# Half of a look-up's lowest-bit picks made by ScalarE in 16-bit halves, and second-level gate sums traced earlier

## The chip, the cores and the metric

The kernel runs on one core of one Trainium2 chip. The metric is the device time of one execution in microseconds (us). The engines are TensorE (PE in the profile, PEld for its weight loads), VectorE (DVE), ScalarE (ACT), GpSimd (POOL) and SyncE (SP). Each has its own list of instructions and works it off in order; "ACTq" and "SPq" in the profile are transfers issued from the lists of ScalarE and SyncE.

## The reference

The input x is 2 x 2048 x 512 in fp32. One block of a transformer is computed, attention first:

```
n = layernorm(x)
q, k, v = n Wq, n Wk, n Wv
s = softmax(q^T k / 4)          # per batch, 512 x 512: over features, not tokens
x = x + (s v^T)^T Wo
```

and then a feed-forward part whose weights are stored as indices into a table of 16 fp32 values:

```
n = layernorm(x)
g = n . lut[gate_idx]^T         # gate_idx and up_idx: 1376 x 512
u = n . lut[up_idx]^T
x = x + (silu(g) * u) . lut[down_idx]^T     # down_idx: 512 x 1376
```

So 3 x 1376 x 512 weights have to be looked up before they can be multiplied with. All products are in fp32.

## The kernel before

**Stages.** Attention over features needs only the 512 x 512 products n^T n of each batch, which the first stage (`gram`) accumulates from the 4096 tokens. Small products of 512 x 512 (`Square`, seven half-size products in place of eight, after Strassen and Winograd) turn them into one matrix m for each batch. Then come 32 blocks of 128 tokens in which y = n m is made: `y_product(k)` is four matmuls, the transposed normalised block nT(k) being their weights. After that `GateUp(f, p)` makes the gate and up products for 128 of the 1376 rows (f from 0 to 10) and 1024 tokens (p from 0 to 3), again in seven or so products a unit, and `Down` makes the last product.

**The order is written out by hand.** TensorE, VectorE, ScalarE and SyncE execute their instructions in the order in which the program's text calls them. What is called one after the other for one engine stays so on that engine, and an instruction that waits holds up all that is behind it on its engine.

**The y stage.** The loop over k calls, in this order: `n_turned(k + 1)` (VectorE transposes the next block, L738, so nT is made one block ahead), `y_product(k)`, `side(k)` and `pump`. `side(k)` calls `added(k - 1)`: VectorE adds y to x and sums the row (L761), ScalarE makes the mean (L164) and the sum of squares (L165, and a read of the accumulator) out of it; after each fourth block a root (L169). Then come, for an earlier block, the transposed copies of the second layernorm (L738 again, from k = 16 on), seven small VectorE operations that finish the layernorm of four blocks (once in four blocks), and `f_normed(k - 6)`: ScalarE normalises a block (L231), and after every second one issues the transfer that stores two of them (L220).

**The look-up.** A `Job` stands for 128 rows of one of the three index matrices, and there are 33 (g, u and wd, each 0 to 10), in a fixed order. ScalarE casts the indices to int16 (`cast`, L251), and VectorE does the rest: it masks out bits 1, 2 and 3 of the index (L263, L264, L269), spreads bit 0 over the word (L267), makes eight picks by bit 0 of the values of two neighbouring entries each, in one bitwise operation (L277), and joins them by seven predicated copies (L289), four of which go by bit 1, two by bit 2 and one by bit 3. `pump(us)` is called between TensorE's products and hands out as many of these operations as the given time allows, by written-down costs. So the pace of the look-up is set by where TensorE stands in the program's text.

**Gate and up units.** A unit calls a1, c1, extra1, the last unit's a4, a2, extra2, c2, b and a3 with `between()`, that is a pump, in between. a1 and c1 are copied out of PSUM by ScalarE (p1 at L932, p7 at L938), so is a2 (u2, L943); VectorE adds c2 to u2, makes the gate's sum h0, and c22 from the unit's accumulator and p7 (L135). ScalarE applies silu to h0 (L1002) and, after a4, to h1 (L1018). a4 of a unit is put between products of the next, and it overwrites the accumulator that c22 reads, so a4 waits for c22.

**Second level.** For f = 2 to 9 two neighbouring f share a second level of the same scheme. Its left sums, s1 to s4 of two gate blocks (`l2_left`, four VectorE operations on 128 x 128), are called ahead of unit (f, 1) for even f, and unit (f, 1)'s extra product into the PSUM tile x reads them.

```
if 1 < f < NFT - 1 and f % 2 == 0 and p == 1:
    for op in l2_left(f):
        op()
```

Of the kernel before, what the change touches and what calls it, by code (L numbers as in the profile page):

```python
# [48 lines left out]
F32 = mybir.dt.float32  # L49
BF16 = mybir.dt.bfloat16  # L50
I32 = mybir.dt.int32
I16 = mybir.dt.int16
# [14 lines left out]
def tile_attn_ffn(  # L67
# [43 lines left out]
    lut_sb = const.tile([P, NLUT], F32, tag="lut", name="lut_sb")  # L111
    lut_x = const.tile([P, NLUT // 2], I32, tag="lutx", name="lut_x")
    eps_sb = const.tile([P, 1], F32, tag="eps", name="eps_sb")
    lut_i = lut_sb.bitcast(I32)
    wd = wdp.tile([P, NFT, E], F32, tag="wd", name="wd")
    nd = dram.tile([NCH, P, KB, J, P], F32, tag="nd", name="nd")
# [21 lines left out]
    class Norm:  # L138
        def __init__(self, c, name, back=None):
            self.name, self.back = f"{name}{c}", back  # L140
            if back:
                self.std, self.mean = back.rstd, back.nmr
            self.rstd = const.tile([P, J], F32, tag=f"rstd_{self.name}", name=f"rstd_{self.name}")
            self.nmr = const.tile([P, J], F32, tag=f"nmr_{self.name}", name=f"nmr_{self.name}")
            self.minus, self.scale = -1.0, 1.0
# [90 lines left out]


    class Job:
        def __init__(self, name, rows, cols, load, dest, after, gate):
            self.name, self.rows, self.cols = name, rows, cols  # L240
            self.load, self.dest, self.after, self.gate = load, dest, after, gate
# [13 lines left out]
            return t[: self.rows, : self.cols]  # L255

        def ops(self):

            rows, f, idx, b3 = self.rows, self.cols / 1024, self.idx, self.b3
            vec = nc.vector  # L260
            w = self.dest()
            b1, b2 = self.bits("b1", 1), self.bits("b2", 1)
            vec.tensor_scalar(b1, b3, 2, None, ALU.bitwise_and)  # L263
            vec.tensor_scalar(b2, b3, 4, None, ALU.bitwise_and)  # L264
            yield 0.2 + 0.54 * f

            vec.tensor_scalar(idx, idx, 31, 31, ALU.logical_shift_left, ALU.arith_shift_right)  # L267
            yield 0.1 + 0.55 * f
            vec.tensor_scalar(b3, b3, 8, None, ALU.bitwise_and)  # L269
            yield 0.1 + 0.27 * f  # L270
            masks = [None, b1, b2, b3]

            def pick(level, at, dest):

                if level == 1:
                    k = at // 2
                    vec.tensor_scalar(  # L277
                        dest.bitcast(I32), idx, lut_x[:rows, k : k + 1],
                        lut_i[:rows, at : at + 1], ALU.bitwise_and, ALU.bitwise_xor,
                    )  # L280
                    yield 0.2 + 0.55 * f
                    return
                yield from pick(level - 1, at, dest)
                half = 1 << (level - 1)
                t = gub.tile(
                    [P, 512], F32, tag="pick", name=f"{self.name}_{level}_{at}", bufs=3
                )[:rows, : self.cols]
                yield from pick(level - 1, at + half, t)
                vec.copy_predicated(dest, masks[level - 1], t)  # L289
                yield 0.1 + 1.17 * f  # L290

            yield from pick(4, 0, w)
            yield from self.after()

# [62 lines left out]
        jobs += [gate_job(f), up_job(f), gate_job(f + 1), up_job(f + 1), down_job(5 + f // 2)]  # L357
    jobs += [gate_job(NFT - 1), up_job(NFT - 1), down_job(NFT - 1)]
    assert len(jobs) == 3 * NFT

    def looked_up():

# [11 lines left out]

    lookup = looked_up()
    owed = [0.0]

    def pump(us):

        owed[0] = min(owed[0] + us, 2 * us + 1.0)  # L380
        while owed[0] > 0:
            cost = next(lookup, None)
            if cost is None:
                return
            owed[0] -= cost
# [153 lines left out]
    for c in range(1, NCH):  # L539
        for j in range(J):  # L540
            gram(c, j)
            if c in (CPB - 1, CPB + 1, CPB + 2):
                n_stored()
            if c == 1 and j == 0:
                second(2)
            if c + 1 < NCH and j < 2:
                for i in (2 * j, 2 * j + 1):
                    ln1[c + 1].stats(i, xc[c + 1][:, i, :])
            elif c + 1 < NCH and j == 2:
                ln1[c + 1].sqrt(0, J)  # L550
                pump(0.6)
                ln1[c + 1].rest(0, J)
                pump(0.6)
            elif ahead and c > STORED + 2:
                for op in ahead[:4]:
                    op()
                del ahead[:4]
            else:
                pump(1.9)
            if c == 1 and j == 1:  # L560
                nc.vector.tensor_tensor(
                    lut_x, lut_pairs[:, :, 0], lut_pairs[:, :, 1], ALU.bitwise_xor
                )
            if c == CPB and j == 1:
                gram_out(0)
            if c == CPB + 1 and j == 3:
                wk_sb = load_weight(wk, "a0", "wk_sb")
                wq_sb = load_weight(wq, "a1", "wq_sb")
                wk_ops = right(wk_sb, "wk")
                ahead += wk_ops.todo  # L570
            if c == CPB and j == 3:
                copies = gram_mirror(0)
            if c == CPB + 1 and j == 1:
                for copy in copies:
                    copy()
                g_ops = [left(gs[0], "g_0")]
                ahead += g_ops[0].todo
# [262 lines left out]
    for k in range(NBLK):  # L840
        if k:
            n_turned(k + 1)
        y_product(k)
        if k == 0:
            before[0].a4()
            n_turned(1)
            n_load(1)
        else:
            if k % J == 3 and k // J + 2 < NCH:
                n_load(k // J + 2)  # L850
            side(k)
        pump(1.6 if k < LAG else 1.0)
    pps.release()
    sums.release()
    ffn = tc.alloc_tile_pool(name="ffn", bufs=1, reuse_waits="tile")
# [19 lines left out]
    def l2_left(f):  # L875


        t = wgu.tile([P, 4, P], F32, tag="l", name=f"l_{f}", bufs=1)
        if f == NFT - 1:
            a12 = gu[f]["12"]  # L880
            both, minus = (t[:, q, : FT[f][1]] for q in range(2))
            gu[f]["both"], gu[f]["minus"] = both, minus
            return [
                lambda: add(both, a12[:, 0, :], a12[:, 1, :]),
                lambda: nc.vector.tensor_scalar_mul(minus, a12[:, 0, :], -1.0),
            ]
        a11, a12 = gw[f][:, 2, :], gw[f][:, 3, :]
        a21, a22 = gw[f + 1][:, 2, :], gw[f + 1][:, 3, :]
        s1, s2, s3, s4 = (t[:, q, :] for q in range(4))
        l2a[f // 2] = {"22": a22, "S1": s1, "S2": s2, "S3": s3, "S4": s4}  # L890
        return [
            lambda: add(s1, a21, a22), lambda: sub(s2, s1, a11),
            lambda: sub(s3, a11, a21), lambda: sub(s4, a12, s2),
        ]
# [11 lines left out]
    class GateUp:  # L906
# [14 lines left out]
        def temp(self, tag, bufs=1):  # L921
            t = ffn.tile([P, CH], F32, tag=tag, name=f"{tag}_{self.name}", bufs=bufs)
            return t[: self.rows, :]
# [100 lines left out]
    class Line:  # L1024
# [29 lines left out]
        def flush(self):  # L1054
            self.last.a4()
            self.last.end()
            self.last = None

    todo = []

    def between():
        if todo:
            todo.pop(0)()
            pump(0.3)
        else:
            pump(1.0)

# [192 lines left out]
    for f, p in units:  # L1260
        while f not in gu or 1 < f < NFT - 1 and p and (f | 1) not in whole:
            next(lookup)
        assert p in xs
        if 1 < f < NFT - 1 and f % 2 == 0 and p == 1:
            for op in l2_left(f):
                op()
        if f == NFT - 1 and p == 0:
            assert not todo and next(lookup, None) is None
            x2p.release()
            gub.release()  # L1270
            for name in ("hp0", "dT"):
                hps[name] = tc.alloc_tile_pool(
                    name=name, bufs=1, side="right", reuse_waits="tile"
                )
            hps[0] = hps["hp0"]
            h = Hidden(0)
            todo += by_two(l2_left(f) + down_sums(hps["dT"]))
        if f == NFT - 1 and p == 1:
            h.rest_of()
            todo += by_two(h.sums())  # L1280
        if f == NFT - 1 and p == 3:
            units = [Down(h, 0)]
        line.run(GateUp(f, p), final=(f, p) == (NFT - 1, NPR - 1))
        if p == NPR - 1:
            passed[0] = f + 1
        if (f, p) == (1, 1):
            xnp.release()
            x2p = tc.alloc_tile_pool(name="x2p", bufs=1, side="right", reuse_waits="tile")
        if f == 1 and p % 2:
            todo += l2_sums(p // 2)  # L1290
# [84 lines left out]
```

## Time and profile before

| | us |
|---|---|
| median of 3 runs (lowest, highest) | 1086.42 (1086.38, 1086.46) |
| the profiled execution | 1086.16 |
| its span, first to last instruction | 1084.2 |
| TensorE busy in it | 1076.2 |
| VectorE busy | 769.2 |
| ScalarE busy | 331.2 |
| GpSimd busy | 35.6 |

The granted TensorE clock is 1.000 over the span. By stage, from the trace: up to 178 us (gram and squares) VectorE is busy for 140.5 us and ScalarE for 75.8; from 178 to 292 us (the y stage) for 100.6 and 60.0 of 114; from 292 to 790 us (gate and up) for 418.6 and 148.4 of 498; after that (down) for 109.5 and 47.0 of 294. TensorE's idle time over the whole span is 8.0 us.

A line of the groups names a line of the program, the engine and operation, output and inputs, shape and count; then the busy time in all and the mean of one in ns; then the engine's idle time just before these instructions and what ended it. A line of the timeline has the start, the duration, the engine and the operation, and in brackets the idle time before it. Durations overlap: an instruction's successor on VectorE or ScalarE often starts before the reported end.

### The profile page before, as it was taken

What the parts mean: (1) busy time and instruction counts of PE and PEld (TensorE: products, weight loads), DVE (VectorE), ACT (ScalarE), POOL (GpSimd) and SP (SyncE); (2) the same over time, 40 slices, a digit from 0 to 9 for tenths busy, and PEclk for the clock granted to TensorE, in tenths of its full rate; (3) what the DMA queues carried; (4) which work ended last, traced back from release to release, by engine and by line L of the source; (5) the groups of instructions that cost most, each with busy time, mean ns of one, the idle gap of its engine ahead of it and who ended that gap; (6) DMA issues with size and microseconds to landing.
All of it is one profiled execution on the core that took longest, in us unless ns stands there. A gap on an engine that the chain in (4) does not pass through costs nothing.

```text
span 1084.2 us, 10362 instructions
## 1 busy us (share of the span) xinstructions
PE 1076.2 (99%) x3442; PEld 644.5 (59%) x3442; DVE 769.2 (71%) x1654; ACT 331.2 (31%) x615; POOL 35.6 (3%) x70
## 2 busy tenths in 40 slices
PE   9999999999999999999999999999999999999998
PEld 5668886444444444444444444444348888888887
DVE  7888777899898778998897897887653334433341
ACT  4652522554632223323332322232221111111110
POOL 0000000012110000000000000000000000000000
PEclk9999999999999999999999999999999999999999
DMA  8750314598661111121111121111415544345421
GB/s 345 227 165 14 84 40 97 136 232 208 171 155 49 48 50 67 59 68 49 59 62 54 59 68 54 53 52 49 148 54 172 172 154 160 98 144 180 155 69 40
DMA packets 87606, 117.15 MB, mean 108 GB/s; under 512 B 14192, under 2 KB 50288, under 8 KB 86656
## 3 DMA queue, kind: packets, MB, share of 16 engines
q1 hardware_dynamic: 62496, 83.39, 24.3%
q0 software_dynamic: 4992, 16.32, 6.1%
q10 hardware_dynamic: 20064, 16.78, 4.8%
q8 instruction: 27, 0.44, 0.2%
q14 instruction: 27, 0.22, 0.1%
HBM read 68.76 MB, written 47.71 MB: 107 GB/s over the span
## 4 chain that ended last, share of the span: by engine, by line
PE 90%; DVE 6%; ACT 2%; issue 1%; ACTq 0%; DMA 0%; SPq 0%; DVEq 0%
PE a_g L899 26%; PE a_d L899 14%; PE c_g L899 13%; PE y L754 8%; PE c_d L899 7%; PE gp L438 4%; PE b_d L899 4%; PE x_g L899 2%; PE b_g L899 2%; PE ea_t L591 1%; PE ea_p L591 1%; PE ea_m L591 1%; PE y_g L899 1%; PE ea_s L591 1%; PE ec_m L591 1%
## 5 line engine op out<-in xcount | busy, mean ns | idle before, releaser
L754 PE MATMUL y<-m,nT 128*128 128x512 f32 x256 | 110.5, 592 | 0.0
L135 DVE TENSOR_TENSOR u<-c_g,u 128x512 f32<-128x512 f32 (+1 forms) x44 | 30.4, 691 | 81.8 <-PE c_g L899 81.7
L754 PEld LDWEIGHTS y<-m,nT 128*128 128x128 f32 x256 | 48.5, 190 | 60.8 <-issue 57.1
L1002 ACT ACTIVATE h<-h 128x512 f32<-128x512 f32 (+1 forms) x44 | 27.7, 630 | 184.1 <-DVE h L135 184.1
L899 PE MATMUL a_g<-xb,wg 128*128 128x512 f32 (+1 forms) x176 | 82.7, 592 | 0.0
L899 PE MATMUL c_g<-xb,wu 128*128 128x512 f32 (+1 forms) x176 | 82.7, 592 | 0.0
L899 PE MATMUL a_g<-xb,s 128*128 128x512 f32 (+1 forms) x176 | 82.7, 592 | 0.0
L899 PE MATMUL a_g<-xT_a,s 128*128 128x512 f32 (+1 forms) x176 | 82.7, 592 | 0.0
L438 PE MATMUL gp<-xn_a 128*128 128x128 f32 (+3 forms) x256 | 70.1, 434 | 1.2 <-DVE xn_a L176 0.8
L899 PE MATMUL a_g<-xT_sq,s 128*128 128x512 f32 (+1 forms) x132 | 62.0, 592 | 0.0
L438 PEld LDWEIGHTS gp<-xn_a 128*128 128x128 f32 x256 | 43.9, 190 | 28.0 <-issue 15.1
L899 PEld LDWEIGHTS a_g<-xb,s 128*128 128x128 f32 (+1 forms) x176 | 33.0, 187 | 42.6 <-issue 37.7
L899 PEld LDWEIGHTS c_g<-xb,wu 128*128 128x128 f32 (+1 forms) x176 | 33.0, 188 | 42.5 <-issue 42.0
L899 PEld LDWEIGHTS a_g<-xT_a,s 128*128 128x128 f32 (+1 forms) x176 | 33.0, 188 | 42.5 <-issue 42.5
L899 PEld LDWEIGHTS a_g<-xb,wg 128*128 128x128 f32 (+1 forms) x176 | 33.0, 188 | 42.5 <-issue 42.3
L289 DVE COPY_PREDICATED wd<-b_wd,wd 128x512 f32<-128x512 int16 (+1 forms) x77 | 56.3, 731 | 1.5
L899 PE MATMUL a_d<-dT,hs_a 128*128 128x256 f32 x224 | 56.2, 378 | 0.0
L135 DVE TENSOR_TENSOR r<-r,a_d 128x256 f32<-128x256 f32 x32 | 13.5, 422 | 53.6 <-PE a_d L899 53.6
L899 PEld LDWEIGHTS a_d<-dT,hs_a 128*128 128x128 f32 x224 | 42.4, 189 | 6.0
L277 DVE TENSOR_SCALAR wd<-idx_wd,lut_x,lut_sb 128x512 int32<-128x512 int32 (+1 forms) x88 | 44.4, 535 | 0.0
L899 PEld LDWEIGHTS a_g<-xT_sq,s 128*128 128x128 f32 (+1 forms) x132 | 24.8, 188 | 31.9 <-issue 31.6
L1018 ACT ACTIVATE h<-a_g 128x512 f32<-128x512 f32 (+1 forms) x44 | 26.2, 596 | 53.3 <-PE a_g L899 53.3
(281 smaller groups left out, 1938.2 us busy)
## 6 DMA issues: line engine op xcount, KB each, us to landing
hd<-h SPq DMA_DIRECT2D x80, 256.0 KB, 2.0
h<-hd SPq DMA_DIRECT2D x40, 512.0 KB, 6.4
nl<-nd SPq DMA_DIRECT2D x32, 256.0 KB, 5.6
xnd<-xn_f ACTq DMA_DIRECT2D x16, 512.0 KB, 5.9
fl<-xnd POOLq DMA_DIRECT2D x32, 256.0 KB, 6.5
xn_back<-xnd SPq DMA_DIRECT2D x32, 256.0 KB, 3.8
out_dram<-r SPq DMA_DIRECT2D x31, 256.0 KB, 2.9
x<-in_x_dram SPq DMA_DIRECT2D x7, 1024.0 KB, 13.4
```

Source lines behind the costliest of these rows:

```text
L135: nc.vector.tensor_tensor(dest, a, b, ALU.add)
L277: vec.tensor_scalar(dest.bitcast(I32), idx, lut_x[:rows, k : k + 1], lut_i[:rows, at : at + 1], ALU.bitwise_and, ALU.bitwise_xor,)
L289: vec.copy_predicated(dest, masks[level - 1], t)
L438: nc.tensor.matmul(gp[b][i][:, i * P :], xn[:, i, j % 2, :], xn[:, i:, j % 2, :], start=c % CPB == 0 and j == 0, stop=c % CPB == CPB - 1 a ...
L591: nc.tensor.matmul(ps[:, m, :], self.a[a][:, k, m * P : (m + 1) * P], self.b[b][:, k, :], start=first and m == k == 0, stop=k == 1, skip_g ...
L754: nc.tensor.matmul(ys[k], nTs[k][:, i, :], m[:, i, :], start=(i == 0), stop=(i == KB - 1))
L899: nc.tensor.matmul(ps, lhsT, rhs, start=first and i == 0, stop=i == len(pairs) - 1, skip_group_check=not first,)
L1002: nc.scalar.activation(h0, h0, AF.Silu)
L1018: nc.scalar.activation(self.h1, self.a, AF.Silu)
```

## The change

For the 29 jobs after the first four, `shared_ops` takes the place of `vector_ops`. Bit 0 is masked out as a tile b0 of its own. VectorE makes picks 0, 4, 8 and 12; picks 2, 6, 10 and 14 are made by ScalarE, each as two operations that write the lower and the upper 16 bits of each fp32 word as an integer: bias + scale x b0, with bias the entry's half (`lut_h`) and scale the difference to the next entry's (`lut_d`), both read as one value a partition. The predicated copies by bit 1 (`with_scalars`) read these tiles, k1, of which there are two. The 232 halves wait in a list, `scalar_ops`. Each pump first calls one of them (two in the y stage) if its pick is at most two ahead of the copies already called; a copy whose halves haven't been called calls them itself. Two small VectorE operations in the gram stage make lut_h and lut_d.

Also, the four sums of `l2_left(f)` are now called at unit (f, 0), in the first `between()` without other work at which gate block f + 1 is looked up, and ahead of the next unit at the latest.

The diff, without the renaming of the temporary tiles of `vector_ops`:

```diff
+    lut_h = const.tile([P, NLUT, 2], F32, tag="luth", name="lut_h")
+    lut_d = const.tile([P, NLUT // 2, 2], F32, tag="lutd", name="lut_d")
...
         def ops(self):
+            return self.shared_ops() if self.scalar else self.vector_ops()
+
+        def shared_ops(self):
+            rows, idx, b3 = self.rows, self.idx, self.b3
+            vec = nc.vector
+            w = self.dest()
+            b0, b1, b2 = self.bits("b0", 1), self.bits("b1", 1), self.bits("b2", 1)
+            made, read = {}, [0]
+
+            def halves(n, at):
+                def half(h):
+                    if h == 0:
+                        made[n] = [temp("k1", 2), 0]
+                    d = made[n][0].bitcast(I16).rearrange("p (c h) -> p c h", h=2)
+                    nc.scalar.activation(
+                        d[:, :, h], b0, AF.Identity, bias=lut_h[:rows, at, h : h + 1],
+                        scale=lut_d[:rows, at // 2, h : h + 1],
+                    )
+                    made[n][1] += 1
+
+                return [(lambda: n < 2 + read[0], lambda h=h: half(h)) for h in range(2)]
+
+            def temp(tag, bufs=1):
+                t = gub.tile([P, 512], F32, tag=tag, name=f"{tag}_{self.name}", bufs=bufs)
+                return t[:rows, : self.cols]
+
+            def own(at, dest):
+                k = at // 2
+                vec.tensor_scalar(
+                    dest.bitcast(I32), idx, lut_x[:rows, k : k + 1],
+                    lut_i[:rows, at : at + 1], ALU.bitwise_and, ALU.bitwise_xor,
+                )
+
+            def with_scalars(n, dest):
+                while n not in made or made[n][1] < 2:
+                    scalar_ops.pop(0)[1]()
+                vec.copy_predicated(dest, b1, made[n][0])
+                read[0] += 1
+
+            vec.tensor_scalar(b0, b3, 1, None, ALU.bitwise_and)
+            vec.tensor_scalar(b1, b3, 2, None, ALU.bitwise_and)
+            for n, at in enumerate((2, 6, 10, 14)):
+                scalar_ops.extend(halves(n, at))
+            yield 0.54
+            vec.tensor_scalar(b2, b3, 4, None, ALU.bitwise_and)
+            vec.tensor_scalar(b3, b3, 8, None, ALU.bitwise_and)
+            yield 0.54
+
+            vec.tensor_scalar(idx, idx, 31, 31, ALU.logical_shift_left, ALU.arith_shift_right)
+            yield 0.4
+            own(0, w)
+            yield 0.5
+            t4, t8 = temp("k2"), temp("k3")
+            own(4, t4)
+            yield 0.5
+            own(8, t8)
+            yield 0.5
+            with_scalars(0, w)
+            yield 0.7
+            with_scalars(1, t4)
+            yield 0.7
+            vec.copy_predicated(w, b2, t4)
+            yield 0.7
+            t12 = temp("k2")
+            own(12, t12)
+            yield 0.5
+            with_scalars(2, t8)
+            yield 0.7
+            with_scalars(3, t12)
+            yield 0.7
+            vec.copy_predicated(t8, b2, t12)
+            yield 0.7
+            vec.copy_predicated(w, b3, t8)
+            yield 0.7
+            yield from self.after()
...
+    for job in jobs[4:]:
+        job.scalar = True
...
-    def pump(us):
-
+    scalar_ops = []
+
+    def pump(us, scalar=1):
+        for _ in range(scalar):
+            if scalar_ops and scalar_ops[0][0]():
+                scalar_ops.pop(0)[1]()
         owed[0] = min(owed[0] + us, 2 * us + 1.0)
...
             if c == CPB and j == 1:
+                nc.vector.tensor_copy(
+                    lut_h, lut_sb.bitcast(I16).rearrange("p (e h) -> p e h", h=2)
+                )
+                by_entry = lut_h.rearrange("p (k two) h -> p k two h", two=2)
+                sub(lut_d, by_entry[:, :, 1, :], by_entry[:, :, 0, :])
...
             side(k)
-        pump(1.6 if k < LAG else 1.0)
+        pump(1.6 if k < LAG else 1.0, 2)
...
+    sums_of = []
     todo = []

     def between():
         if todo:
             todo.pop(0)()
             pump(0.3)
+        elif sums_of and (sums_of[0] | 1) in whole:
+            for op in l2_left(sums_of.pop()):
+                op()
         else:
             pump(1.0)
...
-        if 1 < f < NFT - 1 and f % 2 == 0 and p == 1:
-            for op in l2_left(f):
+        if 1 < f < NFT - 1 and f % 2 == 0 and p == 0:
+            sums_of.append(f)
+        elif sums_of:
+            for op in l2_left(sums_of.pop()):
                 op()
```

More of the change, by code (lines that the diff above doesn't have):

```diff
@@ L238, in tile_attn_ffn @@
     class Job:
+        scalar = False
         def __init__(self, name, rows, cols, load, dest, after, gate):
@@ L259, in ops, with vector_ops @@
+        def vector_ops(self):
             rows, f, idx, b3 = self.rows, self.cols / 1024, self.idx, self.b3
@@ L285, in pick @@
                 t = gub.tile(
-                    [P, 512], F32, tag="pick", name=f"{self.name}_{level}_{at}", bufs=3
+                    [P, 512], F32, tag="k" + str(level - 1), name=f"{self.name}_{level}_{at}",
+                    bufs=2 if level == 2 else 1,
                 )[:rows, : self.cols]
@@ L563, in tile_attn_ffn @@
                 )
+            if c == CPB and j == 1:
+                nc.vector.tensor_copy(
[3 more added lines that the diff above has]
+                sub(lut_d, by_entry[:, :, 1, :], by_entry[:, :, 0, :])
             if c == CPB and j == 1:
```

## The prediction

> **What bounds the kernel now.** I read the page's busy times first, then TensorE's waits, then the groups of the operations that the change touches, and last the timeline at two places where VectorE and ScalarE hand work to and fro.
>
> ```profile
> PE 1076.2 (99%) x3442; PEld 644.5 (59%) x3442; DVE 769.2 (71%) x1654; ACT 331.2 (31%) x615; POOL 35.6 (3%) x70
> ```
>
> TensorE is idle for 8.0 of 1084.2 us. Taking work off VectorE can pay only inside these 8 us. What it waits for:
>
> ```profile
> PE x_g L899 <- DVE l L132: 1.6, 4, 0.5
> PE idle L418 <- POOL ident masks.py:199: 1.4, 1, 1.4
> PE gp L438 <- DVE xn_a L176: 0.8, 1, 0.8
> PE ea_s L591 <- ACT a L612: 0.3, 1, 0.3
> PE c_g L899 <- ACT p L938: 0.2, 1, 0.2
> ```
>
> Only the first line (second-level sums, late four times) is touched for the better. The durations (mean ns before the last bar):
>
> ```profile
> L277 DVE TENSOR_SCALAR wd<-idx_wd,lut_x,lut_sb 128x512 int32<-128x512 int32 (+1 forms) x88 | 44.4, 535 | 0.0
> L231 ACT ACTIVATE xn_f<-x,nmr_f,rstd_f 128x512 f32<-128x512 f32 x32 | 25.4, 801 | 2.1 <-DMA xnd<-xn_f 2.1
> L165 ACT ACTIVATE junk_f<-x,mv_f 128x512 bf16<-128x512 f32 x32 | 23.1, 722 | 1.1
> L251 ACT CAST b_g<-idx_g 128x512 int16<-128x512 int32 (+1 forms) x11 | 6.6, 602 | 1.2 <-ACT xn_f L231 0.6 <-ACT n L231 0.6
> ```
>
> One y block in the timeline: add, mean, squares, normalising, store, next transpose.
>
> ```profile
> 204.37 0.73 DVE L289 COPY_PREDICATED wd<-b_wd,wd 128x512 f32<-128x512 int16 x1
> 204.99 0.99 DVE L277 TENSOR_SCALAR wd<-idx_wd,lut_x,lut_sb 128x512 int32<-128x512 int32 x2
> ...
> 207.18 0.69 DVE L761 SCALAR_TENSOR_TENSOR x<-y,x 128x512 f32<-128x512 f32 x1 [0.59 <-PE y L754]
> 207.92 0.20 ACT L164 ACTIVATE mv_f<-total 128x1 f32<-128x1 f32 x1 [1.34 <-DVE x L761]
> 208.15 0.72 ACT L165 ACTIVATE junk_f<-x,mv_f 128x512 bf16<-128x512 f32 x1
> 208.78 0.18 ACT L165 ACTIVATION_READ_ACCUMULATOR junk_f<-x,mv_f 128x1 f32 x1
> 208.87 1.50 DVE L289 COPY_PREDICATED wd<-b_wd,wd 128x512 f32<-128x512 int16 x2
> 208.87 0.80 ACT L231 ACTIVATE xn_f<-x,nmr_f,rstd_f 128x512 f32<-128x512 f32 x1
> 209.70 0.56 ACTq L220 DMA_DIRECT2D xnd<-xn_f  x1
> 210.26 0.70 DVE L738 STREAM_TRANSPOSE nT<-nl 128x512 f32<-128x512 f32 x1
> ```
>
> VectorE's look-up goes on while ScalarE does its chain; neither waits for the other after the add. VectorE's slack is small: it waits 0.59 us for y in a block of 3.43 us.
>
> **Part 1: second-level sums earlier.** A wait takes the 0.5 us shown or more and a slower restart: in the first, TensorE should have gone on at 394.78 + 4 x 0.43 = 396.50, began at 397.14, and took 1.13 for two products that take 1.02 elsewhere: 0.75. The four come to 0.75 + 0.59 + 0.70 + 0.70 = 2.74 us. With the sums a unit (some 12 us) earlier all of it goes: **-2.7**. Next late on TensorE there is nothing; the sums (four of 0.28) lie beside its products. If the gate block isn't ready, they come where they stood: gain 0.
>
> **Part 2: busy time.** 116 picks of 0.535 leave VectorE, 29 operations of 0.28 (b0) come: some -54 us busy, worth nothing by itself, since TensorE waits for VectorE elsewhere only in the gram stage (0.8, where the jobs stay as they were) and once for 0.3 in the y stage. ScalarE gets 232 halves. No row shows one. Bounds: 0.60 (L251, a cast to int16, no value a partition) and 0.80 (L231, scale and bias both read as one value a partition, as in a half). I take 0.80, the same kind of operation: +186 us, 331 to 517 of 1084, which alone would hide beside TensorE. A successor starts 0.09 before the reported end (208.15 + 0.72 against 208.78), so a pair takes 0.71 + 0.80 = 1.51; at 0.60 it is 1.11.
>
> The Trainium skill (ScalarE: Activation LUTs, "What ACT_TABLE_LOAD costs") gives 186 ns + 0.833 ns an element, and 93 ns for each operand read as one value a partition: 0.80 for a half, as in L231, and by it the sum below stays; with one such operand the same formula gives 0.71, where L165 shows 0.722. Its "Rules for kernel authors" tells to put add and mul on VectorE, not ScalarE. That speaks against the change: a pick is one 0.535 operation there, two of 0.80 here. By that rule alone nothing is lost while ScalarE is idle two thirds of the time, and the time would be that of part 1, 1083.4; the rows of the timeline say that the order decides.
>
> **Part 3: the new wait in the y stage.** Here lies most of the sum. In blocks 9 to 12 and 15 the predicated copy and the pair of halves that it reads are called by the same pump. On ScalarE the pair then stands behind mean, squares, normalising and, each second block, the store of this block, which wait for VectorE's add. On VectorE the copy holds up the next transpose nT, which TensorE needs, and the next add, on which ScalarE's next chain waits. So a loop takes the place of two lists side by side. From the rows: add to mean 0.74; mean to normalising 0.95 (0.33 more with the root); normalising 0.71, with the store 1.39; pair 1.51; hand-over 0.06; copy 0.62 to the next start (204.37 to 204.99), of two dependent ones 1.39 (208.87 to 210.26); transpose 0.62, to its end 0.70.
> Block 9: add 207.18, mean 207.92, normalising 208.87, store over 210.26, pair done 211.77, copy, transpose 212.45, done 213.15. y(11) is due at 213.75: no loss.
> Block 10: add 213.07, mean 213.81, normalising 214.76, pair 215.47 to 216.98, copy and dependent copy, transpose done 219.13. y(12) is due at 217.18: **+1.95**.
> Block 11: add 219.05, normalising and store until 222.13, pair done 223.64, transpose done 225.02; due 222.56: **+2.46**.
> Block 12: add 224.94, root, normalising at 226.96, pair done 229.18, three dependent copies, transpose done 232.10; due 228.45: **+3.65**.
> Blocks 13 and 14 have no such copy (block 14's pair stands ahead of the mean) and catch up: transposes at 235.1 and 238.1, in time. Block 15: mean 238.94, store over 241.28, pair done 242.79, transpose done 244.17; due 242.39: **+1.8**.
> Later copies come to a pair from the pump before, or with at least 0.3 us to spare (y(20)). Sum **+9.9**; with pairs of 1.11 each step is 0.4 earlier, accumulating: 1.15 + 2.06 + 3.25 + 1.25 = 7.7.
>
> **Part 4: gate and up.** In units (5,0), (7,0) and (9,0) the next up job starts early in the unit. For (7,0), from its rows before (silu h1 at 627.89, c2 done 631.39, a4 of (7,0) at 637.13): silu, two halves to 629.91, copy u2, three more halves to 632.5; second predicated copy 631.88, sum u2 632.50, h1 633.12, copy 633.74, h0 634.36 and 635.05 (each waits for the one before), pick 635.10, silu h0 from 635.78, a half to 637.10, third copy 637.16, c22 637.78 to 638.46. Before, c22 started at 636.11. a4 waits **1.33**, the same in (5,1); (9,1) works on 384 columns, 0.9 by the share of the halves. Sum **+3.6**; at 0.60 a half 0.5 + 0.5 + 0.3 = 1.3. Other units have a slack of 0.1 to 0.35 by the same walk.
>
> **Part 5: the rest.** In unit (0,0), c2 waits for p7's copy already (0.2 in the list of waits); a half of 0.71 now stands ahead of it: **+0.6** (0.4 at 0.60). Two tiny VectorE operations in the gram stage: nothing, seven like them take 1.06 in a y block. Index fetches on GpSimd's queue: idx is free no later than before. Stores on ScalarE's queue issue up to 10 us later, as does TensorE; their loads follow some blocks behind.
>
> **Sum**, against the profiled 1086.16: 1086.16 - 2.74 + 9.9 + 3.6 + 0.6 = 1097.5. The runs' median is 0.26 above that execution, nothing beside the sum's error: forecast **1097**.
>
> **Rivals.**
> A. Halves are as short as a cast: 1086.16 - 2.74 + 7.7 + 1.3 + 0.4 = 1092.8. For it: input and output are int16; against it: both per-partition reads.
> B. The y stage loses, gate and up don't, because VectorE arrives there earlier than my rows of before say (54 us lighter): 1097.5 - 3.6 = 1093.9. Against it: TensorE's position paces the pumps, so lists don't run ahead.
> C. Not slower: ScalarE gets to the pairs of blocks 9 to 12 ahead of the block's add, as in block 14, so that copies find them ready. Then parts 3 and 4 vanish: 1086.16 - 2.74 + 0.6 = 1084.0, or 1083.4 without part 5. It decides where a block's loop (5.3 to 6.9 us above) is no longer than 3.43 plus the slack carried in, 0.6. Against it: without any pair the loop still takes 0.74 + 0.95 + 0.71 + 0.06 + 0.62 + 0.62 = 3.7, as long as the order is the written one.
> D. Small slacks go too: units (1,1), (4,0), (6,0) and (8,0), with 0.1 to 0.35 spare, each late by half a half (0.4), and the 2.1 us that ScalarE waits on a store's landing (L231's row) coming into the loop: 1097.5 + 1.6 + 2.1 = 1101.2, twice that wait 1103.3.
>
> **How the numbers follow.** The walk as written 0.50 (1094 to 1100), A 0.15, B 0.12, C 0.09, D 0.14. The range leaves out C and the upper end of D: 1088 to 1103; its lower end allows for A and B together with half the y stage's loss, 1086.16 - 2.74 + 3.85 + 0.4 = 1087.7. About 0.2% (2.2 us) is what a measurement tells from no change: C is split into 0.06 faster and 0.03 same, 0.03 more to same for a y stage that nearly hides; the rest is slower.
>
> **What would show it.** In the profile after: TensorE waits for nT four times, 1.8 to 3.7 us each, between 217 and 245 us, and in y blocks 9 to 12 VectorE's copies by bit 1 wait for ScalarE's k1; halves with a mean near 0.80, 232 of them; a4's products waiting for c22 in (5,1), (7,1), (9,1); no x_g wait on the sums; VectorE some 715, ScalarE some 515 busy. A half at 0.60 means A; no wait on nT means C. I am wrong if the copies' waits end on something other than the halves, or the loop lets go after one block.

## The result, and the profile after

The changed kernel takes 1119.36 us (median; 1118.01 to 1122.41) against 1086.44 in the runs beside it: 1.0307 times as long, 95% interval 1.0286 to 1.0328. The profiled execution took 1122.41 and is the slowest of the four; its span is 1120.6 us (1084.2 before), its granted clock 0.992 (0.995 in the other three). The forecast was 1097 with a range of 1088 to 1103: the sign is right, the size is a third of what came.

The busy times on the page of the kernel after:

```profile
PE 1089.1 (97%) x3442; PEld 645.6 (58%) x3442; DVE 728.9 (65%) x1569; ACT 508.3 (45%) x847; POOL 35.0 (3%) x70
```

VectorE has 40 us less work (54 were forecast), ScalarE 177 more (186 were), and neither is near full. TensorE has the same 3442 products and is busy for 13 us longer with them. What it waits for after:

```profile
PE y L851 <- DVE nT L835: 9.1, 5, 2.4
PE a_g L996 <- DVE c L137: 6.8, 5, 2.4
PE x_g L996 <- ACT r L1069: 6.1, 4, 2.3
PE a_g L996 <- ACT u L1040: 1.4, 1, 1.4
PE c_g L996 <- ACT p L1035: 0.5, 1, 0.5
PE a_g L996 <- ACT p L1029: 0.5, 1, 0.5
```

The wait of the x product on the sums (1.6 before) is gone. In its place stand the transposes nT, as forecast, c22, as forecast but larger, and ScalarE's copies out of PSUM (r, u, and two of p), of which only that of c2 on p, 0.5, was forecast. VectorE's largest waits on ScalarE, with no counterpart before:

```profile
DVE k_wd L300 <- ACT k_wd L278: 34.3, 23, 3.8
DVE k_u L300 <- ACT k_u L278: 24.3, 25, 1.9
DVE k_g L300 <- ACT k_g L278: 24.2, 21, 2.4
DVE wu L300 <- ACT k_u L278: 11.4, 7, 3.4
```

With one smaller group (wd, 2.4) the copies by bit 1 wait 97 us for halves. A half takes 0.95 us, not 0.80:

```profile
L278 ACT ACTIVATE k_wd<-b_wd,lut_h,lut_d 128x512 int16<-128x512 int16 x80 | 71.4, 948 | 5.9 <-ACT xn_f L233 3.6 <-DVE wd L300 2.3
```

VectorE's own operations are hardly longer beside the halves: a predicated copy of wd takes 732 ns before and after, a pick 535 and 540.

Block 10 of the y stage in the timeline after:

```profile
214.43 0.65 DVE L858 SCALAR_TENSOR_TENSOR x<-y,x 128x512 f32<-128x512 f32 x1
215.13 0.20 ACT L166 ACTIVATE mv_f<-total 128x1 f32<-128x1 f32 x1 [1.98 <-DVE x L858]
215.36 0.72 ACT L167 ACTIVATE junk_f<-x,mv_f 128x512 bf16<-128x512 f32 x1
...
216.08 0.80 ACT L233 ACTIVATE xn_f<-x,nmr_f,rstd_f 128x512 f32<-128x512 f32 x1
216.79 1.75 ACT L278 ACTIVATE k_wd<-b_wd,lut_h,lut_d 128x512 int16<-128x512 int16 x2
218.57 0.73 DVE L300 COPY_PREDICATED k_wd<-b_wd,k_wd 128x512 f32<-128x512 int16 x1 [3.47 <-ACT k_wd L278]
219.33 0.73 DVE L325 COPY_PREDICATED wd<-b_wd,k_wd 128x512 f32<-128x512 int16 x1
219.96 0.70 DVE L835 STREAM_TRANSPOSE nT<-nl 128x512 f32<-128x512 f32 x1
...
220.71 1.55 PE L851 MATMUL y<-m,nT 128*128 128x512 f32 x3 [2.45 <-DVE nT L835]
```

This is the loop of the prediction, link by link: add, mean, squares, normalising, two halves, copy, dependent copy, transpose, product; only the pair takes 1.75 us, not 1.51.

The trace allows the whole difference to be split. From one product's start to the next, 512 columns take 0.429 us at the full clock; what is over goes to "half rate" where the product itself lasts longer, to "restart" (0.1) where it is the second after a wait, and to "wait" otherwise:

| us over full pace, profiled executions | wait | restart | half rate |
|---|---|---|---|
| y stage, before | 0.2 | 0.1 | 0.0 |
| y stage, after | 10.0 | 0.5 | 3.4 |
| gate and up, before | 2.7 | 0.5 | 0.0 |
| gate and up, after | 18.9 | 2.0 | 5.0 |

The differences come to 26.0 + 1.9 + 8.4 = 36.3 of the 36.4 us by which the spans differ; the other stages differ by less than half a microsecond.

### The profile page after: what moved, and what is told of

Read it like the earlier page. It is cut to its first block, busy times and chain, and to the rows that moved or that the text cites. A ratio compares the mean times of both kernels' runs of the same rounds, so it can differ in the third digit from the quotient of the medians.

```text
span 1120.6 us, 10522 instructions
## 1 busy us (share of the span) xinstructions
PE 1089.1 (97%) x3442; PEld 645.6 (58%) x3442; DVE 728.9 (65%) x1569; ACT 508.3 (45%) x847; POOL 35.0 (3%) x70
## 4 chain that ended last, share of the span: by engine, by line
PE 73%; ACT 14%; DVE 9%; issue 3%; ACTq 1%; DMA 0%; DVEq 0%; SPq 0%
PE a_g L996 20%; PE a_d L996 14%; PE c_g L996 8%; PE c_d L996 7%; PE y L851 5%; PE gp L528 4%; PE b_d L996 4%; ACT k_u L278 3%; ACT k_g L278 2%; ACT k_wd L278 2%; PE b_g L996 2%; PE x_g L996 1%; DVE h L137 1%; PE ea_t L688 1%; PE ea_m L688 1%
## 5 line engine op out<-in xcount | busy, mean ns | idle before, releaser
L851 PE MATMUL y<-m,nT 128*128 128x512 f32 x256 | 114.9, 609 | 9.1 <-DVE nT L835 9.1
L278 ACT ACTIVATE k_wd<-b_wd,lut_h,lut_d 128x512 int16<-128x512 int16 (+1 forms) x88 | 78.6, 948 | 5.9 <-ACT xn_f L233 3.6
L278 ACT ACTIVATE k_g<-b_g,lut_h,lut_d 128x512 int16<-128x512 int16 (+1 forms) x72 | 64.8, 939 | 5.0 <-DVE b_g L303 3.2
L278 ACT ACTIVATE k_u<-b_u,lut_h,lut_d 128x512 int16<-128x512 int16 (+1 forms) x72 | 62.7, 931 | 0.8 <-DVE b_u L303 0.8
L996 PEld LDWEIGHTS a_g<-xb,wg 128*128 128x128 f32 (+1 forms) x176 | 33.2, 188 | 42.8 <-issue 42.8
L1305 ACT COPY p_d<-a_d 128x256 f32<-128x256 f32 x16 | 6.0, 372 | 90.1 <-PE a_d L996 90.1
L300 DVE COPY_PREDICATED k_wd<-b_wd,k_wd 128x512 f32<-128x512 int16 (+1 forms) x33 | 24.1, 732 | 34.8 <-ACT k_wd L278 34.3
```

Source lines behind the costliest of these rows:

```text
L278: nc.scalar.activation(d[:, :, h], b0, AF.Identity, bias=lut_h[:rows, at, h : h + 1], scale=lut_d[:rows, at // 2, h : h + 1],)
L300: vec.copy_predicated(dest, b1, made[n][0])
L851: nc.tensor.matmul(ys[k], nTs[k][:, i, :], m[:, i, :], start=(i == 0), stop=(i == KB - 1))
L996: nc.tensor.matmul(ps, lhsT, rhs, start=first and i == 0, stop=i == len(pairs) - 1, skip_group_check=not first,)
L1305: nc.scalar.copy(p1, self.a)
```

## Experiments

Theory 1: the halves cost time because of where the written order puts them: the last of them is called by the pump that also calls the copy which reads it, so on ScalarE it stands behind work that waits for VectorE, and copies that TensorE needs stand behind it. Counted in the written order, that is so for 80 of the 116 copies by bit 1. Rival 2: ScalarE's added time counts, wherever it stands. Rival 3: the earlier sums are part of the loss.

**The parts apart.** First the sums alone, in the kernel before (the same edit as in the change):

```diff
-        if 1 < f < NFT - 1 and f % 2 == 0 and p == 1:
-            for op in l2_left(f):
+        if 1 < f < NFT - 1 and f % 2 == 0 and p == 0:
+            sums_of.append(f)
+        elif sums_of:
+            for op in l2_left(sums_of.pop()):
```

> The kernel before with the second-level sums called at unit (f, 0), nothing else. Theory 1 (the loss is TensorE's waits for ScalarE's halves and for what stands behind them; the sums are a gain of their own): the four waits of the x product on the sums go, 2.7 us, and the time is 1083.7. Rival (the earlier sums hold up VectorE in unit (f, 0) and are part of the loss): 1086.4 or more, with new waits of a4 on c22 there.

Measured: 1083.79 us, ratio 0.9977 (0.9968 to 0.9986). In its waits the x product is missing, and no other line of gate and up is over 0.2 us. Theory 1's number was 1083.7; rival 3 falls here. Then the change without them (these lines the other way round):

> The changed kernel with the second-level sums back ahead of unit (f, 1). Theory 1: 1119.4 + 2.7 = 1122, or less where the sums' waits fall together with waits that are there anyway; no less than 1119. Rival (the sums' new place causes part of the loss): below 1117.

Measured: 1132.45, ratio 1.0427 (1.0413 to 1.0441). Rival 3 (below 1117) falls again, but theory 1's 1122 is missed too, by 10 us. TensorE's largest wait in this kernel:

```profile
PE x_g L996 <- DVE l L134: 12.0, 4, 3.7
```

Where VectorE waits for halves, the sums behind those waits come 3 us late in place of 0.4. The early sums are worth 2.4 us before the halves and 13 with them: the parts don't add.

**The stages apart.**

```diff
-    for job in jobs[4:]:
+    for job in jobs[4:10]:
         job.scalar = True
```

> The changed kernel with ScalarE's halves only in jobs 4 to 9 (wd0 to wd5, which are looked up from the squares to the end of the y stage); the later jobs stay on VectorE. Theory 1: the y stage loses as it does in the changed kernel, 13.1 us against before (10.0 of waits for nT, 3.9 of products at half rate, less what was idle before), gate and up only gain the sums' 2.7: 1086.4 + 13.1 - 2.7 = 1097. If the two stages' losses hang together (a late y stage makes gate and up late): above 1105.

and with `jobs[10:]`:

> The changed kernel with ScalarE's halves only from job 10 on (the g, u and wd looked up in gate and up; g2 begins at the end of the y stage). Theory 1: the y stage is as before, and gate and up lose 23.1 us as in the changed kernel: 1086.4 + 23.1 = 1109.5. If the two stages hang together: below 1103.

Measured: 1095.28 (ratio 1.0087, 1.0072 to 1.0103) and 1105.53 (1.0176, 1.0156 to 1.0195). The stages lose by themselves: against the sums alone 11.5 and 21.7, together 33.2 of the 35.6 by which the changed kernel is above them. Executions of the second fall into two sets: 1102.58 and 1103.39 at a granted clock of 1.000, 1107.66 and 1107.81 at 0.995. With the same instructions, the times differ by 4 to 5 us, about what a clock of 0.995 costs over 1105 us (0.005 x 1105 = 5.5). The one that was profiled (1103.39) has waits of up to 2.5 us and hardly a product at half rate.

**What a half costs.** Five forms in one kernel:

```diff
-                    nc.scalar.activation(
-                        d[:, :, h], b0, AF.Identity, bias=lut_h[:rows, at, h : h + 1],
-                        scale=lut_d[:rows, at // 2, h : h + 1],
-                    )
+                    if n == 0:
+                        nc.scalar.activation(d[:, :, h], b0, AF.Identity, bias=bias, scale=scale)
+                    elif n == 1:
+                        nc.scalar.activation(flat, b0, AF.Identity, bias=bias, scale=scale)
+                    elif n == 2:
+                        nc.scalar.activation(d[:, :, h], b0, AF.Copy, bias=3.0, scale=2.0)
+                    elif h == 0:
+                        nc.scalar.activation(made[n][0], b0, AF.Identity, bias=bias, scale=scale)
+                    else:
+                        nc.scalar.activation(made[n][0], idx, AF.Identity, bias=bias, scale=scale)
```

(`flat` is h x 512 elements into the tile, without gaps.)

> What makes a half take 0.95 us and not the 0.80 of the normalising. The changed kernel, its halves in five forms, by which the picks have wrong values: pick 2 as it is (int16, every second element written, two values a partition); pick 6 the same, written without gaps; pick 10 with constants for bias and scale; pick 14's first with an fp32 result without gaps, its second with the int32 index as input and an fp32 result. If the gaps cost it, pick 6's form takes 0.80; if the int16 result does, pick 6's form stays at 0.95 and the fp32 one takes 0.80; if the values read a partition do, only pick 10's form falls, to 0.60 or 0.75. The time is near the changed kernel's, 1110 to 1122, and tells nothing by itself.

Groups of this kernel for the wd jobs, 128 rows (L281 as in the change, L283 without gaps, L285 with constants, L287 fp32 result, L289 from the int32 index); the second number after the bar is the mean in ns:

```profile
L281 ACT ACTIVATE k_wd<-b_wd,lut_h,lut_d 128x512 int16<-128x512 int16 x20 | 18.5, 953 | 1.2 <-ACT xn_f L233 1.2
L283 ACT ACTIVATE k_wd<-b_wd,lut_h,lut_d 128x512 int16<-128x512 int16 x20 | 15.0, 799 | 0.6 <-ACT xn_f L233 0.6
L285 ACT ACTIVATE k_wd<-b_wd 128x512 int16<-128x512 int16 x20 | 14.9, 771 | 3.1 <-DVE wd L308 2.5 <-ACT xn_f L233 0.6
L287 ACT ACTIVATE k_wd<-b_wd,lut_h,lut_d 128x512 f32<-128x512 int16 x10 | 8.1, 806 | 1.2 <-ACT xn_f L233 1.2
L289 ACT ACTIVATE k_wd<-idx_wd,lut_h,lut_d 128x512 f32<-128x512 int32 x10 | 8.1, 812 | 0.3
```

The gaps cost 0.15 us a half (953 against 799). Input and output types cost nothing here, and the two values read a partition about 0.18 (953 against 771; that form also goes by Copy in place of Identity, which was not tried by itself). So the nearest row, 0.80, was right for a half's work and left out how it is written. One execution of this kernel took 1106.10 us, less than the 1110 to 1122 expected: three quarters of its operations are shorter than the changed kernel's halves.

Now that size alone, in the changed kernel's own order:

```diff
-                        d[:, :, h], b0, AF.Identity, bias=lut_h[:rows, at, h : h + 1],
-                        scale=lut_d[:rows, at // 2, h : h + 1],
+                        made[n][0].bitcast(I16)[:, h * self.cols : (h + 1) * self.cols], b0,
+                        AF.Identity, bias=lut_h[:rows, at, 1:2], scale=lut_d[:rows, at // 2, 1:2],
```

> The changed kernel in its own order (80 of 116 in the copy's pump), the halves written without gaps, so that one takes 0.80 us as my prediction had it, not 0.95 (both halves are made of the upper 16 bits, so the picks have wrong values). If the size of a half was what my sum had wrong, the time is the predicted 1097.5. If the sum missed waits in gate and up (copies out of PSUM behind halves), it is 1103 to 1112.

Measured: 1104.21 (1.0165, 1.0148 to 1.0182), the second case. TensorE's waits here:

```profile
PE y L851 <- DVE nT L835: 8.8, 4, 3.3
PE a_g L996 <- DVE c L137: 4.3, 4, 1.6
PE x_g L996 <- ACT r L1069: 3.2, 3, 1.2
```

Split as above: y stage 9.5 of waits, gate and up 10.5, half rate 0.1 in all. So 0.15 us a half are worth 15.2 us of the change's 33, and with halves of the predicted size 20.4 remain against the sums alone. Between the two profiled executions, 18.4 us apart, it is 8.9 of waits, nearly all in gate and up, and 8.3 at half rate.

**Order against ScalarE's time.** One operation with an fp32 result in place of two halves:

```diff
-                        d[:, :, h], b0, AF.Identity, bias=lut_h[:rows, at, h : h + 1],
-                        scale=lut_d[:rows, at // 2, h : h + 1],
+                        made[n][0], b0, AF.Identity, bias=lut_sb[:rows, at : at + 1],
+                        scale=lut_d[:rows, at // 2, 0:1],
...
-                return [(lambda: n < 2 + read[0], lambda h=h: half(h)) for h in range(2)]
+                return [(lambda: n < 2 + read[0], lambda h=h: half(h)) for h in range(1)]
```

> The changed kernel, but ScalarE makes each pick in one operation with an fp32 result (bias the entry, scale the difference to the next, from b0) in place of two int16 halves: 116 operations, not 232, with the same two tiles and one call a pump. In the written order the last of a copy's operations is called in the copy's own pump for 16 of 116 copies, in the changed kernel for 80. Theory 1 (what counts is whether the operations are called with the copy that reads them, and so stand behind work that waits for VectorE): most waits go, 1085 to 1092. Rival 2 (ScalarE's added time counts, in proportion): it falls from 208 to some 95 us, so the loss of 36 us against the early sums alone (1083.8) falls to 16: 1100.

Measured: 1083.70 (0.9977, 0.9968 to 0.9987): the whole loss is gone, better than theory 1's own range. This moved both the order and ScalarE's time (409.6 us busy), so each was then moved alone. ScalarE's time, by issuing each operation twice:

```diff
                     made[n] = [temp("k1", 2), 1]
+                    for _ in range(1):
+                        nc.scalar.activation(
+                            made[n][0], b0, AF.Identity, bias=lut_sb[:rows, at : at + 1],
+                            scale=lut_d[:rows, at // 2, 0:1],
+                        )
```

> The kernel with one operation a pick, each operation issued twice in a row: ScalarE is busy with 232 operations of 0.81 us again, near what the halves take, while the order stays that of one operation a pick (16 of 116 copies read a pick called in their own pump). Theory 1 (place in the order): little is lost against 1083.7, 1084 to 1091. Rival 2 (ScalarE's time): most of the loss comes back, 1108 to 1118.

Measured: 1089.48 (1.0028, 1.0017 to 1.0039), ScalarE busy for 496.4 us, nearly as in the changed kernel. The order, by taking the early calls out of the pump:

```diff
-        for _ in range(scalar):
-            if scalar_ops and scalar_ops[0][0]():
-                scalar_ops.pop(0)[1]()
```

> The kernel with one operation a pick, none of them called ahead by a pump: each is called by the copy that reads it (116 of 116 in the copy's own pump). ScalarE's time is that of one operation a pick, 95 us. Theory 1: VectorE waits at every one of these copies, the y stage and gate and up lose again, 1098 to 1112. Rival 2: as with one operation a pick, 1084 to 1086.

Measured: 1108.65 (1.0205, 1.0189 to 1.0220), with ScalarE busy for 409.4 us. Its y stage waits longer than the changed kernel's:

```profile
PE y L843 <- DVE nT L827: 13.2, 9, 2.6
PE a_g L988 <- DVE c L136: 2.5, 4, 0.8
```

The same two hundred-odd operations cost 6 us where they are called early; half their number costs 25 where they are called with their copy. At last the changed kernel with its own halves, called earlier in gate and up:

```diff
-    def pump(us, scalar=1):
+    def pump(us, scalar=2):
```

> The changed kernel with one number changed: two halves called a pump everywhere, as in the y stage, not one. The same 232 halves of 0.95 us and the same two tiles; 20 of 116 copies have a half called in their own pump. The order of the y stage stays. Theory 1: gate and up lose much less than 23 us, 1095 to 1106, with the y stage's loss left. Rival 2: 1115 to 1122, ScalarE being as busy.

Measured: 1102.84 (1.0151, 1.0136 to 1.0166). The split shows gate and up at 7.0 us of waits in place of 18.9; the y stage, whose order is the same but for one half called earlier at its start, still has 8.9. One number in the order of the calls is worth 16.5 us at the same 508.3 us of ScalarE's time. Rival 2 falls; that its time counts a little where a wait is near, the doubled operations' 6 us show. What calling the halves still further ahead would give is not shown: with four tiles for the picks in place of two, which up to four picks ahead need, the kernel doesn't fit (its pool x2p needs 20 KB a partition, some 16 are left). Nor was the y stage run with its halves called earlier; that its loss goes with the order is shown there by the kernels with one operation a pick: TensorE doesn't wait in that stage where they are called early, and waits 13.2 us where they are called late.

**What a wait of TensorE costs.** Extra transposes in the kernel before:

```diff
         if k:
+            for _ in range({9: 5, 13: 5, 17: 5, 21: 6, 25: 6, 29: 7}.get(k, 0)):
+                turn(sums.tile([P, KB, P], F32, tag="g", name=f"late_{k}", bufs=1), nls[(k + 1) // J][:, (k + 1) % J])
             n_turned(k + 1)
```

> What a wait of TensorE costs by itself. The kernel before, with five to seven extra transposes of 0.62 us (into a tile that nothing reads) ahead of nT in blocks 9, 13, 17, 21, 25 and 29, so that TensorE waits there once each, some 0.5 to 3 us. If a wait costs only its length and the 0.11 us of the restart, the time is 1086.4 plus the waits and 0.7. If, as the changed kernel's profile has it, waits of 2 us and more can be followed by 3.4 us at half rate, the longer ones among them cost up to 1.7 us more each, and the executions differ by that.

> The same with seven or eight extra transposes at the same places, so that most waits are 2 to 4 us long. Waits alone: 1086.4 plus the waits and 0.7. With stretches at half rate: 1.7 us more for each wait that has one, and nearly all waits over 3 us should have one; of those between 2 and 3 only some.

Measured: 1105.89 (1.0181, 1.0164 to 1.0198; single executions from 1104.51 at a clock of 0.996 to 1108.23 at 0.994) and 1114.90 (1.0259, 1.0244 to 1.0275). In the y stage the first has 16.9 us of waits and 2.3 at half rate, the second 18.9 and 10.0: 2 us more of waiting, 9 us more of time. All four waits over 3 us of the second are followed by a stretch at half rate; in the first one of 3.40 us is not, one of 4.54 is. A wait of 3.36 us in the second, and what follows it, in the windows view (TensorE's busy time first, the granted clock after POOL):

```profile
260.00:264.00 4.00, 0.84 (x2) 0.01 (x1) 3.86 (x7) 0.00 (x0) 0.00 (x0) 0.91 0.24 81
264.00:267.40 3.40, 3.36 (x4) 1.51 (x5) 3.26 (x14) 2.17 (x5) 0.00 (x0) 0.50 0.01 2
267.40:271.00 3.60, 3.60 (x7) 1.39 (x5) 3.57 (x8) 1.90 (x5) 0.64 (x2) 0.62 0.86 230
```

## Why the prediction was wrong

**Part 1, the sums (-2.7):** right; alone they gave 2.4. That a sum late behind VectorE's waits costs far more was not seen, since nothing in the change leaves them there.

**Part 2, a half at 0.80:** mis-sized; 0.95. The row was taken for its operation and operands; the write to every second 16-bit element, in plain sight in the diff, has no row before and got no bound above 0.80. The Trainium skill's formula (ScalarE: Activation LUTs, "What ACT_TABLE_LOAD costs") also gives 0.80 and holds for the form without gaps (0.799); no term of it stands for the gaps. Its rule on add and mul ("Rules for kernel authors") told the right sign, and an operation is indeed longer on ScalarE (0.81 against 0.535 for a pick); but that is not what costs here: with one operation a pick ScalarE has the work at no cost (1083.70 against 1083.79 us). VectorE's -54 us came to -40, at least in part because the rows' means hold the overlap with the next operation (two picks in a row take 0.99); no wait hangs on it.

**Part 3, the y stage (+9.9):** right in mechanism, and in size for the half that the sum used: without gaps TensorE waits 1.99, 2.32, 3.46 and 1.71 us for y(12), y(13), y(14) and y(17), where the walk had 1.95, 2.46, 3.65 and 1.8. That the changed kernel, with halves of 0.95, has 10.0 us of waits is luck. It has a fifth, 0.59 for y(11), and 2.61, 2.55, 2.01 and 2.17 for the others; beside them stand 3.4 us of products at half rate, and half of these took the place of a wait, as VectorE goes on meanwhile. Kernels with the same order in these blocks show it. With halves in jobs 4 to 9 alone, and in the change without the early sums, y(14) waits 3.70 and 3.71 us; in the changed kernel, where 1.8 us were lost at half rate just before, behind the wait for y(13), it waits 2.01. Without the early sums 1.8 us were lost behind the wait for y(12), and y(13) waits 0.87, not 2.55.

**Part 4, gate and up (+3.6, and 0.6 in part 5):** the waits that were walked came as walked, and here the prediction failed all the same, by those that were not. With halves of 0.80 (the kernel without gaps) a4 waits 1.35 in (5,1) and in (7,1), where the walk had 1.33, and 0.45 in (9,1) (0.9); c2 of (0,0) waits 0.57 in all. Beside them stand 6.8 us that the sum has not: 1.77 in (3,3), 1.37, 1.38 and 0.94 for the x product in (4,3), (6,3) and (8,3), 0.80 for a copy u, and 0.55 in three small ones. "Other units have a slack of 0.1 to 0.35 by the same walk" is the step that fell. In unit (3,3) before, c22 (c<-a_g,p) is done 0.59 us before a4 begins (468.75 against 469.34):

```profile
467.12 0.63 ACT L1002 ACTIVATE h<-h 128x512 f32<-128x512 f32 x1 [4.72 <-DVE h L135]
467.88 0.58 ACT L932 COPY p<-a_g 128x512 f32<-128x512 f32 x1
468.07 0.68 DVE L135 TENSOR_TENSOR c<-a_g,p 128x512 f32<-128x512 f32 x1
...
469.34 1.88 PE L899 MATMUL a_g<-xb,s 128*128 128x512 f32 x4
```

The same place in the changed kernel, where the wait of a4 is longest:

```profile
485.50 0.63 ACT L1099 ACTIVATE h<-h 128x512 f32<-128x512 f32 x1 [2.65 <-DVE h L137]
486.04 1.75 ACT L278 ACTIVATE k_g<-b_g,lut_h,lut_d 128x512 int16<-128x512 int16 x2
487.66 0.55 ACT L1029 COPY p<-a_g 128x512 f32<-128x512 f32 x1
487.82 0.73 DVE L300 COPY_PREDICATED k_g<-b_g,k_g 128x512 f32<-128x512 int16 x1 [2.35 <-ACT k_g L278]
488.44 0.68 DVE L137 TENSOR_TENSOR c<-a_g,p 128x512 f32<-128x512 f32 x1
...
489.18 3.08 PE L996 MATMUL a_g<-xb,s 128*128 128x512 f32 x4 [2.35 <-DVE c L137]
```

It is the y stage's loop in another dress: silu waits for h0 from VectorE, the halves stand behind silu, the copy waits for the halves, and c22, for which a4 waits, stands behind the copy. The job is a gate job, where the walk had looked at up jobs. The other kind needs ScalarE alone: the copies r and u out of PSUM, which let the next product into their accumulator, stand behind halves, as here p does. In unit (4,3), where the product began without a wait before:

```profile
546.02 1.76 ACT L278 ACTIVATE k_g<-b_g,lut_h,lut_d 128x512 int16<-128x512 int16 x2
547.64 0.56 ACT L1069 COPY r<-x_g 128x512 f32<-128x512 f32 x1
...
548.25 2.08 PE L996 MATMUL x_g<-xb,l 128*128 128x512 f32 x2 [2.32 <-ACT r L1069]
```

**Half rate:** no term of the sum; 8.4 us in the profiled execution. Every wait was priced at its length. The trace before has no wait over 0.7 us from the y stage on and no product at half rate there; only its first products, at the start, are slow:

```profile
L418 PE MATMUL idle<-ident 128*128 128x512 f32 x6 | 4.8, 967 | 1.4 <-POOL ident masks.py:199 1.4
```

A product of this shape takes 592 ns elsewhere. The row stood in the profile before and could have told that TensorE has a second pace.

**The sum, put right:** 1097.5 + 6.8 (the missed waits at 0.80) = 1104.3, against 1104.21 measured without gaps; the gaps add 15.2 to 1119.4. That it comes out to 0.1 is in part luck: the y stage and the walked waits were some 0.4 and 0.5 us shorter than forecast, and the restarts of all these waits, some 1.4 us, are in no term. The rivals: A (short halves) and C (no loop) were as wrong as they were unlikely; B had gate and up lose nothing, where most of the loss is; D had small slacks used up there, the right place at a fraction of the price. The range was too narrow above because it took the unwalked units for safe.

## What to carry to other kernels

An idle engine does moved work for nothing only if the work is done before its reader needs it. Where something ahead of it in that engine's list waits for the engine it was taken from, the two lists become a loop: call the work at least one step before its reader, and count readers whose operand is called in the same step (80 of 116 here, and 16 where the loss was gone). When one such loop is found in a walk, look for the same form in every stage, and for each instruction behind the moved work ask which product it frees. In this case a wait of TensorE of 2 us and more needs a second price, up to 1.8 us, and up to 2.7 above 3 us; part of it comes back where the next wait is for the same late engine.

## What the runs showed of the hardware

ScalarE writing every second 16-bit element of a row takes 0.95 us for 512 elements, without gaps 0.80 (953 and 799 ns, scale and bias read as one value a partition).

TensorE can fall to half its clock after a wait of little over 2 us. Windows of the kernel after; the second begins behind a wait of 2.55 us, and its clock is 0.54:

```profile
220.00:226.80 6.80, 3.70 (x9) 1.44 (x9) 3.08 (x8) 3.94 (x7) 0.56 (x1) 1.00 0.91 229
226.80:230.20 3.40, 3.40 (x5) 1.39 (x6) 0.54 (x2) 2.77 (x7) 0.00 (x0) 0.54 0.00 0
```

Over the eleven traces with waits of 0.9 us and more, none of 41 waits under 2 us was followed by such a stretch, 10 of 27 between 2 and 3 us were, and 10 of 13 above; the products then lost 1.5 to 2.7 us, mostly the 1.7 to 1.8 of one stretch of 3.4 us. Waits of the same length went both ways (2.61 us at 218 us did in one kernel and did not in three others), so length alone does not decide. The Trainium skill (TensorE: Matmul & The Clock Gate, "Part 1: The HAM clock gate") describes a free-running window of about 3.4 us after which an idle TensorE is halved, which fits the length of the stretches and the chance in them. It does not fit that waits of 2.2 to 2.8 us, too short to fill such a window, were enough; its advice of no gaps over about 3 us ("Why this matters for your kernels") is too lax for this case, where 2.17 us sufficed. What decides between waits of the same length is not shown.
